# Products with 128-column weights in place of pairs of 64: v and two output projections of a MetaFormer kernel

## The chip, the core and the metric

The kernel runs on one core of a Trainium2 chip. The core has a matrix engine (TensorE, PE in the profile, with its weight loads listed apart as PEld), a vector engine (DVE), a scalar engine (ACT), GpSimd (POOL) and a sync engine (SP) that issues DMAs. Each engine works through its own queue in order; semaphores tie the queues together. The metric is the device time of one launch in microseconds, taken as the median of several runs.

A TensorE product has two operands: the weights, which a load instruction brings into the array, and the moving operand, which is streamed past them. The number of columns of the weights is the number of output partitions. The array can be used whole (weights of 128 rows by 128 columns, written 128*128 in the profile) or split into tiles, for example two halves of 64 columns each (128*64), which hold different weights.

## The reference

Input x has 32 images of 56x56 positions and 96 channels. Two layers follow, each an attention or scan part and then a feed-forward part:

```python
x = x + conv0(_ln_c(x))                  # attention in windows of 7x7, shifted by 3
t = t + ffn0(_ln_t(t))                   # rounded to fp8 and fp16, 96 -> 384 -> 96
x = x + conv1(_ln_c(x))                  # gated scan along the width
t = t + ffn1(_ln_t(t))
```

In the attention, `qkv = xs @ w_qkv + b_qkv` gives q, k and v with 3 heads of 32; each window of 49 tokens attends to itself, and the result goes through `out @ w_out + b_out`. In the scan part, a layer norm is followed by `x @ W_expand` and `sigmoid(x @ W_gate)` (192 channels each), a linear recurrence over the 56 columns of each row, the product of gate and scan, and `gated @ W_out` (192 to 96 channels). All of these are in float32.

## The kernel before

**Blocks.** Work is cut into blocks of 14 image rows, two rows of windows, 784 tokens: 4 blocks an image (NBLK), 128 in all. A block's activations `xb` lie with tokens on partitions: partitions 0 to 55 hold one image row, 64 to 119 another, and 7 such pairs of rows (G) lie side by side, each with 96 channels.

**Steps and ticks.** Each block goes through some 90 named steps (`LD`, `ma`, `q`, `v`, `pr`, `so`, ...). The string `PIPELINED` lists the steps with a lag: in tick t, step `name:lag` is run for block t - lag. A tick so has every step once, each on another block, and the steps of one engine stay in the order of this text (`in_order` ties them). The scan steps SC0 to SC5 run once for each image, spread over four ticks. TensorE's steps of a tick in order are: k, (a scan), v, pr, q, te, hf2, sc, pu2, pu1, gt1, gt0, av, hf1, tg, pu0, pu3, so, ta, tro, (scans), tf, hg2, yg, yf, hf0, hg0, hg1. The PSUM memory is used as four slots of two banks (`banks`); a slot is given back at the step that `EMPTIES` names, and that assignment is made when the program is written, not while it runs.

**The three products that change.** All contract over 128 partitions, of which 96 are channels and one is a row of ones for the bias; the other weight or activation rows are zero.

- *v* (L630 to L641). `xws` holds the normed input of the attention, channels on partitions, tokens in the order of windows: 16 windows of 49 tokens one behind the other, and 15 words of padding at the end (OVER). For each window the weights are 64 consecutive words from the window's start (49 tokens and the first 15 of the next window), the moving operand is the 96 columns of the v part of `wqkv`, and the result goes to partitions 0 to 63 or 64 to 127 of `pv`. That is 16 products a block. `xws` is written by the step `ea` (L600 to L606), two ACT copies that turn image order into window order, and is read as the moving operand by `q` and `k` (L609 to L622).
- *pr* (L785 to L795). `ot` holds the attention's output, channels on partitions, 14 rows of 56 tokens one behind the other. For each image row the weights are 64 words from the row's start, the moving operand is `wo` (96 columns), and rows of even and odd number go to the lower and upper half of the partitions. That is 14 products a block. `ot` is written by `eo` (L775 to L783).
- *so* (L985 to L998). `gTs` holds the gated scan turned to channels on partitions, 14 rows of 64 words (56 tokens and 8 of padding), in two halves of 96 channels each (h). For each row and each h there is one product, the two h adding up in PSUM. That is 28 products a block.

After v, ACT copies the result to `vs` (`ev`); after pr and so, DVE adds the result to `xb` (`ad`, `as`). A float32 product shows in the profile as two passes, each with a weight load and a matmul, so that the counts there are twice those above.

Of the kernel before, what the change touches and what calls it, by code (L numbers as in the profile page):

```python
# [8 lines left out]
F32 = mybir.dt.float32  # L9
# [8 lines left out]
C = 96  # L18
HW = 56
WS = 7  # L20
# [9 lines left out]
TP = 2 * HW  # L30
ROW = 64
# [3 lines left out]
G = 7  # L35
NBLK = 4
NTOK = G * TP
NPAIR = 8
W2 = WS * WS
OVER = 64 - W2  # L40
# [47 lines left out]
def kernel(  # L88
# [27 lines left out]
    nc = tc.nc  # L116
# [3 lines left out]
    const = ctx.enter_context(tc.tile_pool(name="const", bufs=1))  # L120
# [7 lines left out]
    def banks(name):  # L128

        slot = free.pop(0)  # L130
        (taken if tracked else free).append(slot)
        return psum.tile([128, 2, 512], F32, tag=f"ps{slot}", name=name)
# [24 lines left out]
    def zeros(size, name, first=0):  # L157
        t = const.tile([128, size], F32, name=name)
        nc.gpsimd.memset(t[first:], 0.0)
        return t  # L160
# [11 lines left out]
    for iy in range(WS):  # L172
# [12 lines left out]
    wo = zeros(C, "wo", C)  # L185

    weg = zeros(2 * E, "weg", C).rearrange("p (h m) -> p h m", h=2)
    wso = zeros(2 * C, "wso", C).rearrange("p (h c) -> p h c", h=2)
# [7 lines left out]
        fill=1.0,  # L196
# [225 lines left out]

    xws, vs, gTs, xqs = [], [], [], []
    for n in range(2):
        xws.append(const.tile([128, NTOK + OVER], F32, name=f"xw_{n}"))
        xqs.append(const.tile([128, NTOK], F8, name=f"xq_{n}"))
        vs.append(const.tile([128, NPAIR * NH, HD + 1], F32, name=f"v_{n}"))
        gTs.append(const.tile([128, 2, 8 - 2 * n, ROW], F32, name=f"gT_{n}"))
    ot = const.tile([128, NTOK + ROW - HW], F32, name="ot")
    hqs = [const.tile([128, 2 * G, ROW], F8, name=f"hq_{n}") for n in range(6)]  # L430
    qk01 = const.tile([128, 2, HALF + OVER], F32, name="qk01")
    qk2 = const.tile([128, 2, QUARTER + OVER], F32, name="qk2")
# [2 lines left out]
    fill = nc.gpsimd.memset  # L435

    def prepare_attention():
        for n in range(2):
            fill(xws[n][C:, :], 1.0)
            fill(xws[n][0:C, NTOK:], 0.0)  # L440
            fill(vs[n][:, :, HD:], 1.0)
        fill(qk2[:, :, QUARTER:], 0.0)
        fill(qk01[:, :, HALF:], 0.0)
        fill(pT[:, :, HALF:], 1.0)
        fill(ot[:, NTOK:], 0.0)
        fill(ot[C:, :], 1.0)

    ident8 = const.tile([128, TP], F8, name="ident8")

# [35 lines left out]
    def steps(*names):  # L485


        def enter(f):
            if len(names) == 1:
                step[names[0]] = f  # L490
            else:
                for k, n in enumerate(names):
                    step[n] = lambda i, k=k: f(i, k)
            return f

        return enter
# [3 lines left out]
    @steps("R0", "R1", "R2", "R3", "R4", "R5", "R6", "R7")  # L500
    def _(t, k):

        if k == 0:
            held["root", t] = epoch[0]
            epoch[0] += 1
        at = held["root", t] % 2
        st, y, v, a = stats[at], roots[at], variances[at], halfway[at]
        if k == 0:
            nc.vector.scalar_tensor_tensor(v, st[:, :, 0:G, 2], 1.0 / C, shifts, op0=ALU.mult, op1=ALU.add)
        elif k == 1:  # L510
            nc.vector.tensor_scalar(y.bitcast(I32), v.bitcast(I32), -0.5, ROOT_BITS, op0=ALU.mult, op1=ALU.add)
        elif k in (2, 5):
            nc.vector.tensor_tensor(a, y, y, ALU.mult)
        elif k in (3, 6):
            nc.vector.scalar_tensor_tensor(a, a, -ROOT_STEPS[k // 4][0], v, op0=ALU.mult, op1=ALU.mult)
        else:
            nc.vector.scalar_tensor_tensor(y, a, ROOT_STEPS[k // 5][1], y, op0=ALU.add, op1=ALU.mult)  # L517
        if k == 7:
            done[0] = held.pop(("root", t))
# [54 lines left out]
    def out_banks(name):  # L574

        po = banks(name)
        return [
            (g0, g1, po[:, k, 0 : (g1 - g0) * C].rearrange("p (g c) -> p g c", c=C))
            for k, (g0, g1) in enumerate(((0, 4), (4, G)))
        ]  # L580
# [19 lines left out]
    @steps("ea")  # L600
    def _(i):

        order = xws[i % 2][0:C, 0:NTOK].rearrange("c (r w a b) -> c r a w b", r=2, a=WS, b=WS)
        pt = held.pop(("tra", i))
        for r in range(2):
            nc.scalar.copy(order[:, r], pt[:, r].rearrange("c a (w b) -> c a w b", b=WS))  # L606

    @steps("q", "k")
    def _(i, n):  # L609

        parts, h0, h1 = ((2, 0, 2), (4, 2, 3))[n]
        size, rows = NTOK // parts, 128 // parts
        pq = banks(f"qk_{i}_{n}")
        for m in range(2):
            for j in range(parts):
                nc.tensor.matmul(  # L616
                    pq[j * rows : (j + 1) * rows, m, 0:size],
                    wqkv[:, m * C + h0 * HD : m * C + h1 * HD],
                    xws[i % 2][:, j * size : (j + 1) * size],
                    start=True,  # L620
                    stop=True,
                )  # L622
        held["qk", i, n] = pq[:, :, 0:size]
# [6 lines left out]
    @steps("v")  # L630
    def _(i):
        pv = banks(f"pv_{i}")
        for w in range(2 * NPAIR):
            p0, pair = (w % 2) * 64, w // 2
            nc.tensor.matmul(  # L635
                pv[p0 : p0 + 64, pair // 4, (pair % 4) * C : (pair % 4 + 1) * C],
                xws[i % 2][:, w * W2 : w * W2 + 64],
                wqkv[:, 2 * C : 3 * C],
                start=True,
                stop=True,  # L640
            )  # L641
        held["v", i] = pv
# [133 lines left out]
    @steps("eo")  # L776
    def _(i):
        pt = held.pop(("tro", i))
        for r in range(2):
            nc.scalar.copy(  # L780
                ot[0:C, 0:NTOK].rearrange("c (a r w b) -> c r w a b", a=G, r=2, b=WS)[:, r],
                pt[0:C, r].rearrange("c (w s) -> c w s", s=ROW)[:, :, 0:W2].rearrange("c w (a b) -> c w a b", b=WS),
            )  # L783

    @steps("pr")  # L785
    def _(i):
        parts = out_banks(f"pr_{i}")
        held["pr", i] = [(slice(g0, g1), po) for g0, g1, po in parts]
        for g0, g1, po in parts:
            for g in range(g0, g1):  # L790
                for r in range(2):
                    first = g * TP + r * HW
                    nc.tensor.matmul(  # L793
                        po[r * ROW : (r + 1) * ROW, g - g0, :], ot[:, first : first + ROW], wo, start=True, stop=True
                    )  # L795

    step["ad"] = add_out("pr")

# [185 lines left out]
    @steps("so")  # L984
    def _(i):  # L985
        held["so", i] = []
        for gT, (g0, g1, po) in zip(gTs, out_banks(f"so_{i}")):
            held["so", i].append((slice(g0, g1), po))
            for g in range(g1 - g0):
                for h in range(2):  # L990
                    for r in range(2):
                        nc.tensor.matmul(  # L992
                            po[r * ROW : (r + 1) * ROW, g, :],
                            gT[:, h, 2 * g + r, :],
                            wso[:, h, :],
                            start=(h == 0),
                            stop=(h == 1),
                        )  # L998

    step["as"] = add_out("so")  # L1000
    feed_forward("g", 1)
# [17 lines left out]
    def pipeline(text, track, one_bias):  # L1019
# [16 lines left out]
        for t in range(nblocks + 1 + max(lag for _, lag in table)):  # L1036
            if t == scans - NBLK + 1:
                parts.setdefault((t, 0), []).append(turn_toep)
            prepare(*parts.get((t, 0), ()))
            for name, lag in table:  # L1040
                i = t - lag
                if name[0:2] in ("SC", "GA"):
                    due = (i - PHASE[int(name[2])]) % NBLK == 0 and window(i)
                elif name[0] == "R":
                    due = i >= 0
                else:
                    due = (PRELOADED if name == "LD" else 0) <= i < nblocks
                if not due:
                    continue
                step[name](i)  # L1050
                if taken:
                    slots[name, i] = [len(filled[name]), list(taken)]
                    taken.clear()
                if track and name in empties:
                    use = slots[empties[name], i]
                    use[0] -= 1
                    if use[0] == 0:
                        free.extend(use[1])
            prepare(*parts.get((t, 1), ()))
# [59 lines left out]
```

## Time and profile before

| | |
|---|---|
| median of 3 runs | 3170.72 us (3163.45 to 3171.2) |
| the profiled execution | 3165.43 us, span 3163.7 us |
| mean granted TensorE clock | 0.989 |
| busy: PE, DVE, ACT, POOL | 96%, 82%, 73%, 48% |
| chain that ended last | PE 90%, ACT 5%, DVE 2% |
| of it, so (L992), pv (L635), pr (L793) | 10%, 6%, 5% |
| so: passes, mean matmul, mean weight load | 7168, 248 ns, 138 ns |
| pv | 4096, 251 ns, 138 ns |
| pr | 3584, 246 ns, 137 ns |

How to read it: the chain of work follows the last instruction back to what released it, step by step, so a share there is time that set the end. Mean times of a matmul are from its start to its modelled end and overlap with the next ones; the spacing of the starts tells the pace. In the groups, the line of a tile gives engine, operation, out<-in, the shape of the weights (rows*columns), the moving operand (rows x columns), and the number of passes. A name such as `tr_a` is the tile that is written; `pu` is the expansion and gate, `av` the attention's weighted values, `s` its scores, `py` and `ph` the feed-forward products, `tr_*` and `gt` transposes.

### The profile page before, as it was taken

The page shows a single profiled execution, that of the slowest core. Times are in us where ns is not written, and L with a number is a line of the kernel's source. Part 1 is how long each engine was busy: PE and PEld are TensorE (multiplying, and loading weights), DVE is VectorE, ACT ScalarE, POOL GpSimd, SP SyncE. Part 2 cuts the span into 40 slices and gives each one's busy share as a digit, 9 for nine tenths or more (in the row PEclk, how much of TensorE's full clock was granted, in tenths as well). Part 3 has the DMA queues.
Part 4 walks back from the last instruction along what each step waited for, and adds up shares of the span by engine and source line. Part 5 has one row for each costly group of instructions (what it writes and reads, how often), then busy time and mean ns, then how long its engine had stood idle before and what let it go on. Part 6 is the DMA issues. An engine that isn't in the chain of part 4 may idle for free.

```text
span 3163.7 us, 180034 instructions
## 1 busy us (share of the span) xinstructions
PE 3042.9 (96%) x80228; PEld 2511.5 (79%) x80228; DVE 2605.6 (82%) x7149; ACT 2304.8 (73%) x4610; POOL 1504.6 (48%) x1219
## 2 busy tenths in 40 slices
PE   4999999999999999999999999999999999999996
PEld 3778888888888888888888888888888888888875
DVE  6778888888888888888888888888888888888876
ACT  2667777777777777777777777777777777777774
POOL 4555444445444445444444444544544544544540
PEclk8899999999999999999999999999999999999998
DMA  6000111111111111111111111111111111111001
GB/s 140 23 4 19 29 32 27 29 32 27 29 32 27 28 33 27 28 33 26 27 34 27 26 34 27 26 34 27 26 33 28 27 34 27 26 32 29 23 22 34
DMA packets 232640, 97.09 MB, mean 31 GB/s; under 512 B 225292, under 2 KB 231854, under 8 KB 231854
## 3 DMA queue, kind: packets, MB, share of 16 engines
q1 hardware_dynamic: 228410, 84.40, 11.5%
q8 instruction: 633, 10.37, 1.4%
q10 hardware_dynamic: 3444, 1.06, 0.2%
q14 instruction: 153, 1.25, 0.1%
HBM read 42.05 MB, written 43.35 MB: 27 GB/s over the span
## 4 chain that ended last, share of the span: by engine, by line
PE 90%; ACT 5%; DVE 2%; issue 2%; POOL 1%; DVEq 0%; ACTq 0%; DMA 0%; SPq 0%; POOLq 0%
PE pu L896 20%; PE so L992 10%; PE qk L616 9%; PE scan L939 7%; PE av L738 6%; PE pv L635 6%; PE s L658 5%; PE pr L793 5%; PE ph_g L815 4%; PE py_f L849 4%; PE py_g L849 4%; ACT qk L628 3%; PE gt L217 3%; PE ph_f L815 3%; PE tr_f L566 2%
## 5 line engine op out<-in xcount | busy, mean ns | idle before, releaser
L896 PE MATMUL pu<-weg,xs 128*64 128x192 f32 x7168 | 640.9, 330 | 4.1 <-ACT xs L882 3.5
L535 DVE BATCH_NORM_STATS2 stats<-xb 128x6 f32<-128x192 f32 x2048 | 578.1, 348 | 1.8 <-POOL xb L871 1.7
L555 POOL TENSOR_TENSOR xn_f<-xc_f,roots 128x672 fp8e5<-128x672 f32 x128 | 243.4, 1901 | 663.6 <-DVE roots L517 663.6
L896 PEld LDWEIGHTS pu<-weg,xs 128*64 128x64 f32 x7168 | 492.4, 137 | 81.4 <-ACT xs L882 6.0
L871 POOL TENSOR_TENSOR xb<-xb,y_f 128x672 f32<-128x672 f32 x128 | 239.3, 1870 | 464.6 <-DVE y_f L867 461.2
L541 POOL TENSOR_TENSOR xc_f<-xb,stats 128x672 f32<-128x672 f32 x128 | 181.6, 1419 | 426.9 <-DVE stats L535 270.2
L628 ACT COPY qk<-qk 128x392 f32<-128x392 f32 (+1 forms) x256 | 173.8, 679 | 231.9 <-PE qk L616 231.7
L992 PE MATMUL so<-wso,gT 128*64 128x96 f32 x7168 | 322.8, 248 | 4.8 <-ACT gT L982 4.8
L827 ACT CAST h_g<-ph_g 128x784 f16<-128x784 f32 x384 | 307.6, 856 | 27.3 <-PE ph_g L815 16.9
L827 ACT CAST h_f<-ph_f 128x784 f16<-128x784 f32 x384 | 318.4, 829 | 10.4 <-PE ph_f L815 10.4
L992 PEld LDWEIGHTS so<-wso,gT 128*64 128x64 f32 x7168 | 315.9, 138 | 10.2 <-ACT gT L982 5.4
L839 POOL CAST hq<-h_f 128x784 fp8e5<-128x784 f16 x384 | 320.3, 834 | 6.1 <-DVE h_f L833 6.1
L616 PE MATMUL qk<-xw,wqkv 128*32 128x196 f32 (+1 forms) x3072 | 304.8, 392 | 2.3 <-ACT h_f L827 2.3
L606 ACT COPY xw<-tr_a 96x392 f32<-96x392 f32 x256 | 117.4, 514 | 249.1 <-PE tr_a L217 212.6
L586 DVE TENSOR_TENSOR xb<-so,xb 128x384 f32<-128x384 f32 (+1 forms) x256 | 118.1, 503 | 188.8 <-PE so L992 188.8
L586 DVE TENSOR_TENSOR xb<-pr,xb 128x384 f32<-128x384 f32 (+1 forms) x256 | 118.1, 503 | 183.4 <-PE pr L793 183.4
L959 DVE SCALAR_TENSOR_TENSOR gt<-gt,scan 128x448 f32<-128x448 f32 (+2 forms) x694 | 236.5, 400 | 38.3 <-PE scan L939 38.1
L849 PEld LDWEIGHTS <-hq 128*128 128x128 fp8e5 x5376 | 246.7, 99 | 26.4 <-DVE hq L839 8.6
L939 PEld LDWEIGHTS scan<-u,toep 64*64 64x64 f32 x12288 | 200.1, 135 | 64.6 <-ACT xw L606 29.2
L939 PE MATMUL scan<-u,toep 64*64 64x56 f32 (+1 forms) x12288 | 221.6, 220 | 30.8 <-ACT xw L606 21.3
L917 ACT COPY u<-pu 128x384 f32<-128x384 f32 (+1 forms) x512 | 242.1, 473 | 4.5 <-PE pu L896 4.5
L911 ACT ACTIVATE gt<-pu 128x384 f32<-128x384 f32 (+1 forms) x512 | 237.8, 464 | 5.5 <-PE pu L896 5.5
(161 smaller groups left out, 6706.0 us busy)
## 6 DMA issues: line engine op xcount, KB each, us to landing
xb<-in_x_dram SPq DMA_DIRECT2D x224, 126.0 KB
out_dram<-xb SPq DMA_DIRECT2D x224, 126.0 KB
taps_d<-u SPq DMA_DIRECT2D x1, 4704.0 KB
xb<-in_x_dram SPq DMA_DIRECT2D x224, 13.1 KB
xb<-in_x_dram SPq DMA_DIRECT2D x224, 7.9 KB
out_dram<-xb SPq DMA_DIRECT2D x224, 13.1 KB
out_dram<-xb SPq DMA_DIRECT2D x224, 7.9 KB
xb<-in_x_dram SPq DMA_DIRECT2D x32, 72.0 KB
```

The costliest lines, as they stand in the source:

```text
L535: nc.vector.bn_stats(st[:, g : g + 2, :].rearrange("p g s -> p (g s)"), pair.rearrange("p g c -> p c g"))
L555: engine("n" + n).tensor_tensor(xn, xc, rs[:, :, None].to_broadcast([128, G, C]), ALU.mult, **saturate)
L616: nc.tensor.matmul(pq[j * rows : (j + 1) * rows, m, 0:size], wqkv[:, m * C + h0 * HD : m * C + h1 * HD], xws[i % 2][:, j * size : (j + 1) ...
L628: nc.scalar.copy(dst, held.pop(("qk", i, n)))
L827: nc.scalar.copy(h16.rearrange("p (h t) -> p h t", h=2), held.pop(("ph", n, i, hc))[:, :, 0:HALF])
L839: engine(f"c{n}{hc}").tensor_copy(hq[:, :, 0:HW], h16.rearrange("p (r w) -> p r w", w=HW), saturate=False)
L849: nc.tensor.matmul(po[:, g - g0, :], hq[hc][:, 2 * g : 2 * g + 2, :].rearrange("p r w -> p (r w)"), w2q[:, hc, :], start=(hc == 0), stop=( ...
L871: engine("k" + n).tensor_tensor(xtiles[i], xtiles[i], held.pop(("y16", n, i)), ALU.add)
L896: nc.tensor.matmul(pu[h * RS : (h + 1) * RS, g, r * E : (r + 1) * E], xs[:, 2 * j + g, r, :], weg[:, h, :], start=True, stop=True,)
L917: nc.scalar.copy(dst, held["pu", i, j][:, 0:n, :, EH:].rearrange("p g r e -> p e g r"))
L939: nc.tensor.matmul(py[o0 : o0 + RS, b, e, rows], toep[h * RS : (h + 1) * RS, ch * HW : ch * HW + RS], u[h * RS : (h + 1) * RS, ch, rows], ...
L992: nc.tensor.matmul(po[r * ROW : (r + 1) * ROW, g, :], gT[:, h, 2 * g + r, :], wso[:, h, :], start=(h == 0), stop=(h == 1),)
```

## The change

Two tokens' rows, or two windows, are laid side by side at a distance of 64 words, so that 128 consecutive words hold both, and one product with 128-column weights takes the place of two with 64. `xws` gets 16 windows of 64 words (49 tokens and 15 of zeros), `ot` gets 14 rows of 64 words (56 tokens and 8 of zeros); `gTs` had that form already. The copies `ea` and `eo` write into the new places, and `q` and `k` read 49 of each 64 words. v then has 8 products a block, pr 7 and so 14. The order of the steps is as before on every engine, and the other instructions are the same ones; some memsets at the start are larger or smaller.

```diff
-        xws.append(const.tile([128, NTOK + OVER], F32, name=f"xw_{n}"))
+        xws.append(const.tile([128, 2 * NPAIR, 64], F32, name=f"xw_{n}"))
...
-    ot = const.tile([128, NTOK + ROW - HW], F32, name="ot")
+    ot = const.tile([128, 2 * G, ROW], F32, name="ot")
...
-            fill(xws[n][C:, :], 1.0)
-            fill(xws[n][0:C, NTOK:], 0.0)
+            fill(xws[n][C:], 1.0)
+            fill(xws[n][0:C, :, W2:], 0.0)
...
-        fill(ot[:, NTOK:], 0.0)
-        fill(ot[C:, :], 1.0)
+        fill(ot[0:C, :, HW:], 0.0)
+        fill(ot[C:], 1.0)
...
-        order = xws[i % 2][0:C, 0:NTOK].rearrange("c (r w a b) -> c r a w b", r=2, a=WS, b=WS)
+        order = xws[i % 2][0:C, :, 0:W2].rearrange("c (r w) (a b) -> c r a w b", r=2, b=WS)
...
-                    pq[j * rows : (j + 1) * rows, m, 0:size],
+                    pq[j * rows : (j + 1) * rows, m, 0:size].rearrange("p (w s) -> p w s", s=W2),
                     wqkv[:, m * C + h0 * HD : m * C + h1 * HD],
-                    xws[i % 2][:, j * size : (j + 1) * size],
+                    xws[i % 2][:, j * size // W2 : (j + 1) * size // W2, 0:W2],
...
-        for w in range(2 * NPAIR):
-            p0, pair = (w % 2) * 64, w // 2
+        for pair in range(NPAIR):
             nc.tensor.matmul(
-                pv[p0 : p0 + 64, pair // 4, (pair % 4) * C : (pair % 4 + 1) * C],
-                xws[i % 2][:, w * W2 : w * W2 + 64],
+                pv[:, pair // 4, (pair % 4) * C : (pair % 4 + 1) * C],
+                xws[i % 2][:, 2 * pair : 2 * pair + 2, :].rearrange("p w s -> p (w s)"),
                 wqkv[:, 2 * C : 3 * C],
...
-                ot[0:C, 0:NTOK].rearrange("c (a r w b) -> c r w a b", a=G, r=2, b=WS)[:, r],
+                ot[0:C, r : 2 * G : 2, 0:HW].rearrange("c a (w b) -> c w a b", b=WS),
...
-                for r in range(2):
-                    first = g * TP + r * HW
-                    nc.tensor.matmul(
-                        po[r * ROW : (r + 1) * ROW, g - g0, :], ot[:, first : first + ROW], wo, start=True, stop=True
-                    )
+                nc.tensor.matmul(
+                    po[:, g - g0, :], ot[:, 2 * g : 2 * g + 2, :].rearrange("p r w -> p (r w)"), wo, start=True, stop=True
+                )
...
                 for h in range(2):
-                    for r in range(2):
-                        nc.tensor.matmul(
-                            po[r * ROW : (r + 1) * ROW, g, :],
-                            gT[:, h, 2 * g + r, :],
-                            wso[:, h, :],
-                            start=(h == 0),
-                            stop=(h == 1),
-                        )
+                    nc.tensor.matmul(
+                        po[:, g, :],
+                        gT[:, h, 2 * g : 2 * g + 2, :].rearrange("p r w -> p (r w)"),
+                        wso[:, h, :],
+                        start=(h == 0),
+                        stop=(h == 1),
+                    )
```

## The prediction

> **What bounds the kernel now.** I read four views in this order: the page's busy shares and its chain of work, the PE timeline of one steady tick, the groups of weight loads kept apart by shape, and short windows inside single steps. The page first:
>
> ```profile
> PE 3042.9 (96%) x80228; PEld 2511.5 (79%) x80228; DVE 2605.6 (82%) x7149; ACT 2304.8 (73%) x4610; POOL 1504.6 (48%) x1219
> PE 90%; ACT 5%; DVE 2%; issue 2%; POOL 1%; DVEq 0%; ACTq 0%; DMA 0%; SPq 0%; POOLq 0%
> ```
>
> TensorE is both the busiest engine and nine tenths of the chain that ended last. So the length of its steps is what counts. The PE timeline of one tick (start, length of the union, tile, weights rows*columns, moving rows x columns, passes):
>
> ```profile
> 1501.29 2.48 PE L992 MATMUL so<-wso,gT 128*64 128x96 f32 x56
> 1503.70 0.55 PE L217 MATMUL tr_a<-ident,xc_a 56*96 56x56 f32 x14
> ...
> 1506.69 1.05 PE L849 MATMUL py_g<-w2q,hq 128*128 128x96 fp8e5 x21
> 1507.58 1.06 PE L849 MATMUL py_f<-w2q,hq 128*128 128x96 fp8e5 x21
> ...
> 1510.40 1.54 PE L635 MATMUL pv<-wqkv,xw 128*64 128x96 f32 x32
> 1511.77 1.32 PE L793 MATMUL pr<-wo,ot 128*64 128x96 f32 x28
> 1512.92 1.49 PE L616 MATMUL qk<-xw,wqkv 128*64 128x392 f32 x8
> ...
> 1522.01 0.50 PE L566 MATMUL tr_g<-ident,xn_g 128*96 128x112 fp8e5 x7
> 1522.44 2.17 PE L896 MATMUL pu<-weg,xs 128*64 128x192 f32 x24
> ```
>
> The reader is to take step lengths from start to next start: pv 1.37 us, pr 1.15, so 2.41, in all 4.93 us of a tick; a tick is 23.16 (the chain enters so at 1501.46 and again at 1524.62). An f32 product is two passes, each with its own weight load (pv x32 for 16 products). pr has 28 passes in 1.15 us: 82 ns for each pair of half-width passes, which go to the two column halves of the array and run side by side. A pass of 96 columns holds its half for nearly all of that: so's mean matmul is 248 ns, pu's with twice the columns 330, so 96 f32 columns stream for 82. Today's pace is thus set by streaming, and the loads of 64 columns lie under it.
>
> Now the loads, by shape (busy us, mean ns of one):
>
> ```profile
> L849 PEld LDWEIGHTS <-hq 128*128 128x128 fp8e5 x5376 | 246.7, 99 | 26.4 <-DVE hq L839 8.6 <-POOL hq L839 0.2
> L635 PEld LDWEIGHTS pv<-wqkv,xw 128*64 128x64 f32 x4096 | 175.6, 138 | 33.9 <-ACT h_f L827 18.1 <-issue 13.4 <-PE qk L616 0.6
> L616 PEld LDWEIGHTS qk<-xw,wqkv 128*64 128x64 f32 x1024 | 66.1, 137 | 49.7 <-issue 47.1 <-ACT h_f L827 2.5
> L616 PEld LDWEIGHTS qk<-xw,wqkv 128*32 128x32 f32 x2048 | 54.3, 111 | 47.9 <-ACT y_f L861 31.4 <-PE ph_f L815 4.1 <-issue 0.3
> ```
>
> An f32 load grows by 26 to 27 ns for 32 more columns (111 to 137 or 138), so 64 columns take some 53 ns of loading and the rest is latency. No row has an f32 load of 128 columns outside the transposes of the setup. That a load, and not the stream, can set the pace is seen in windows inside av (33 moving columns) and inside a short scan (14 moving columns), a short window beside a long one from the same start, loads counted as x:
>
> ```profile
> 1520.30:1520.50 0.20, 0.20 (x24) 1.00 0.00 0
> 1520.30:1521.30 1.00, 1.00 (x78) 1.00 0.07 16
> 126.40:126.50 0.10, 0.10 (x16) 1.00 0.00 0
> 126.40:127.10 0.70, 0.70 (x56) 1.00 0.00 0
> ```
>
> av: 54 more loads in 0.80 us, 14.8 ns each; both steps use four tiles of the array in turn, so one tile takes a new 64-column load every 59 ns. The scan: 40 in 0.60 us, 60 ns per tile, though its stream is less than half as long as av's. Two steps with unlike streams and one pace: that pace is the load's.
>
> **The change, part by part.** Per block v goes from 32 passes of 64-column weights to 16 of 128, pr from 28 to 14, so from 56 to 28: 58 pairs become 58 full-width passes that follow one another in the undivided array. They compute the same products; the moving side stays 96 f32 columns, 82 ns. The weights per pass are twice as wide.
>
> Pace of a full-width pass. From below it is the stream, 82 ns, if the load hides; from above load and stream in turn. That a load runs under a stream in the undivided array is seen in the setup's transposes (weights of up to 128 f32 columns, moving 128 and 96):
>
> ```profile
> 14.08 0.42 PE L401 MATMUL w1t<-ident,u 128*96 128x128 f32 x1
> 14.08 0.23 PEld L402 LDWEIGHTS w1t<-ident,u 96*128 96x128 f32 x1
> 14.29 0.37 PE L402 MATMUL w1t<-ident,u 96*128 96x96 f32 x1
> ```
>
> The load begins as the matmul ahead of it begins. So I take the larger of stream and load, and the load as the 59 ns of a 64-column tile plus 64 columns at 26.5 ns per 32, 53 ns: **112 ns**. Its near ends are 108 (the overhead beyond 106 almost gone) and 118 (59 doubled). The far ends are 82 and 112+82 = 194.
> - 58 x (112 - 82) = **+1.74 us** a tick.
>
> Changes of tile shape. Seven tr_g passes at 49 ns (the chain gives 0.34 us for seven of them behind matmuls of their own shape) are 0.34 us, but pu, of another shape, starts 0.43 behind: 0.09 us to change. Today v, pr and q share 128*64, and so do pu and so. Afterwards pr to q and pu to so are two more changes: **+0.18 us**.
>
> First loads that nothing hides. v's first load is already bare (1.37 - 16 x 0.082 = 0.06) and grows to 0.11: +0.05. q gets one of 0.06, so one of 0.11: together **+0.22 us**.
>
> The last passes of pr and of so now release the array after a stream of 82 instead of a pace of 112: **-0.06 us**.
>
> The copies ea and eo write runs of seven words before and after, into rows of 64 or 112 with gaps; I take nothing. ea's copy is on the chain between tr_a and the scan (0.52 us a tick), so a tenth more would cost 0.05 us, 7 us in all; a gain has no reason. The moving side of q and k is now 8 or 4 runs of 49 out of 64 in place of one run. I take nothing; above, each run breaking the stream by 2 or 3 ns over four rounds of each gives 0.12 us, 15 us in all. The larger memsets at the start are about 1100 more columns on POOL; 128x5376 took 4.58 us there, so 0.9 us, beside PE's own wait of 11.7 us for xc_a: nothing, at most 1 us. DVE, ACT, SP and the DMAs keep their instructions and order, with no new wait on any queue. Evictions behind v, pr and so (ev, ad, as) start later with PE; they have more room, because a longer tick lowers DVE's and ACT's shares. PE's waits for ACT (21.3 us for xw before the scan) remain, since tr_a comes after so and the copy only then.
>
> Sum: 1.74 + 0.18 + 0.22 - 0.06 = 2.08 us a tick. Every block passes each step once: x 128 = 266 us. All but the first few ticks have PE at nine tenths or more, so I let all of it reach the end. The profiled execution took 3165.4 us (span 3163.7 and 1.7 around it), 5.3 below the median 3170.7 of the three runs, inside their spread of 3163.5 to 3171.2. 3165.4 + 266 = **3431 us**, +8.4%.
>
> A rule that speaks harder against the change, weighed against the rows: the Trainium skill, "TensorE: Matmul & The Clock Gate", Part 3 "The mechanism", says that a weight load overlaps running matmuls only where it goes to another row group. All passes here use all rows, so by it each would pay load and stream, the 194 of rival two, and the time would be about 4040. The rows differ: so's two halves use all rows as well and keep 82 ns for a pair, where load and stream in turn would be 53 + 82 = 135. I go by the rows.
> A rule that speaks for it: "TensorEngine Tiling (Array Packing)", "Feature Incompatibilities", says that column tiling excludes the fast weight load, so the undivided array could win it back; the TensorE page, "Weight-path perf modes", says it is off for FP32. The trace shows only the fp8 side (99 ns for 128 columns). By the first alone the sum would be rival one's.
>
> **The rivals.**
> - One, *the wide load hides*. Full-width fp8 weights load in 99 ns, faster than the 64-column f32 ones at 138, so full width may have a quicker path. Against: that row's type is not f32, and f32 rows grow steadily with columns. Then the pace stays 82 and only shape changes and some bare loads are paid, 0.18 to 0.40 us a tick: 23 to 51 us, about 3205.
> - Two, *load and stream in turn* at 194: 58 x 112 + 340 = 6.84 us a tick, +875, about 4040. Against it stand so's pace and the setup's overlapped loads.
> - Three, *faster*: the undivided f32 pass streams at the pace of py, whose 21 passes of the same 96 columns take 0.89 us, 42 ns each, because the split array is what slows f32. 58 x (42 - 82) + 300 = -2.0 us a tick, -259, about 2907. The point from which it decides is a pace of 76 ns (58 x 6 pays the 0.34 of extras). Against it: py is fp8, and the undivided f32 matmuls of the setup differ by 53 ns for 32 moving columns (421 against 368), no less per column than the split ones.
>
> **How the numbers follow.** Forecast (load sets a pace of 100 to 125 ns: 3340 to 3530): 0.84; within it, 108 to 118 gives 3400 to 3480. Rival one 0.07, two 0.05, three 0.04. The predicted time is the forecast's 3431. The range 3345 to 3505 is paces of 100 to 123, and it leaves out the rivals and the top of the forecast, 2 in 10. Within 0.3%, about what a measurement of this kernel can tell from no change, only the low end of rival one could come: 0.01. Faster 0.04, slower 0.95.
>
> **What would show it.** Right: pv, pr and so at x16, x14 and x28 with 128*128 weights and f32 loads of about 190 ns (138 + 53); loads within a step about 112 ns apart; start to start pv near 1.9 us, pr near 1.6, so near 3.3 up to tr_a; pu x24 to so near 2.1; a tick near 25.2; PE still about nine tenths of the chain, DVE's share down to about 76%. Wrong: passes 82 ns apart in so (rival one), near 190 (two), or at 42 (three). The forecast also fails if q and k lengthen (runs of 49), if the copies at ea grow, or if a slower PE lets ACT's copies come earlier and PE's waits for other engines (some 70 us outside the setup, by the waits view) shrink.

## The result, and the profile after

The changed kernel takes 3426.86 us (median of five runs, 3420.41 to 3430.67) against 3170.72 for the kernel before: a ratio of 1.0804, 95% interval 1.0783 to 1.0825. That is 256 us more; the prediction said 266 more and 3431. The profiled execution has a span of 3424.5 us against 3163.7, 261 more.

The page of the kernel after, the same two lines as before the change (busy time by engine, and the chain that ended last):

```profile
PE 3303.3 (96%) x72804; PEld 2731.2 (80%) x72804; DVE 2608.6 (76%) x7149; ACT 2306.4 (67%) x4610; POOL 1503.7 (44%) x1219
PE 90%; ACT 5%; DVE 2%; issue 2%; POOL 1%; SPq 0%; DVEq 0%; ACTq 0%; DMA 0%; POOLq 0%
```

TensorE issues 7424 fewer matmuls (58 for each of 128 blocks) and is busy for 260 us longer. DVE, ACT and POOL are busy for as long as they were; only their shares fall. The chain has the same shares: nothing else became the bound. Its steps in one tick, from the PE timeline of the kernel after (start, length, line, tile, weights, moving operand, passes):

```profile
1501.21 3.37 PE L988 MATMUL so<-wso,gT 128*128 128x96 f32 x28
1504.50 0.55 PE L217 MATMUL tr_a<-ident,xc_a 56*96 56x56 f32 x14
...
1512.28 2.02 PE L634 MATMUL pv<-wqkv,xw 128*128 128x96 f32 x16
1514.14 1.73 PE L790 MATMUL pr<-wo,ot 128*128 128x96 f32 x14
1515.80 1.54 PE L616 MATMUL qk<-xw,wqkv 128*64 128x392 f32 x8
1517.26 0.55 PE L217 MATMUL tr_e<-ident,xc_e 56*96 56x56 f32 x14
...
1525.36 2.17 PE L893 MATMUL pu<-weg,xs 128*64 128x192 f32 x24
1527.46 2.81 PE L988 MATMUL so<-wso,gT 128*128 128x96 f32 x23
```

From start to next start: so 3.29 us (2.41 before), pv 1.86 (1.37), pr 1.66 (1.15), q 1.46 (1.42), pu0 and pu3 together 2.10 (2.00). That is +0.88, +0.49, +0.51, +0.04 and +0.10: 2.02 us a tick, x 128 = 259 us. A tick with one scan is 25.19 us long in the chain, against 23.16:

```profile
1527.54 3.29 PE so L988 x28
...
1552.73 3.29 PE so L988 x28
```

The 261 us of span are not all steps of the tick. In the profile after, the first k step starts 44.79 us after the span's start, and in the profile before at 38.82: 6 us are lost in the setup. From there to the end the span is 255 us longer, 2.0 us for each of 128 blocks.

The weight loads of the three steps (busy us, mean ns of one, idle before), and a short and a long window inside so (loads as x; the number behind the count is the granted clock):

```profile
L988 PEld LDWEIGHTS so<-wso,gT 128*128 128x128 f32 x3584 | 409.7, 192 | 39.9 <-issue 32.2 <-ACT gT L979 5.4 <-ACT u L914 1.1
L634 PEld LDWEIGHTS pv<-wqkv,xw 128*128 128x128 f32 x2048 | 242.7, 194 | 33.0 <-ACT h_f L824 18.1 <-issue 12.7 <-PE qk L616 0.3
L790 PEld LDWEIGHTS pr<-wo,ot 128*128 128x128 f32 x1792 | 212.3, 193 | 0.4 <-ACT y_f L858 0.4
```

```profile
1501.50:1501.70 0.20, 0.20 (x4) 1.00 0.00 0
1501.50:1504.30 2.80, 2.80 (x27) 1.00 0.03 6
```

A load of 128 f32 columns takes 192 to 194 ns, 55 more than one of 64. In so 23 loads pass in 2.60 us: a pass every 113 ns, where a pair of half-width passes took 82.

### The profile page after: what moved, and what is told of

It reads as the page before. It is cut to its first block, busy times and chain, and to the rows that moved or that the text cites. A ratio compares the mean times of both kernels' runs of the same rounds, so it can differ in the third digit from the quotient of the medians.

```text
span 3424.5 us, 165187 instructions
## 1 busy us (share of the span) xinstructions
PE 3303.3 (96%) x72804; PEld 2731.2 (80%) x72804; DVE 2608.6 (76%) x7149; ACT 2306.4 (67%) x4610; POOL 1503.7 (44%) x1219
## 4 chain that ended last, share of the span: by engine, by line
PE 90%; ACT 5%; DVE 2%; issue 2%; POOL 1%; SPq 0%; DVEq 0%; ACTq 0%; DMA 0%; POOLq 0%
PE pu L893 18%; PE so L988 12%; PE qk L616 9%; PE pv L634 7%; PE scan L936 6%; PE av L737 6%; PE pr L790 6%; PE s L657 5%; PE ph_g L812 4%; PE py_g L846 3%; PE py_f L846 3%; ACT qk L628 3%; PE gt L217 3%; PE ph_f L812 3%; PE tr_f L566 2%
## 5 line engine op out<-in xcount | busy, mean ns | idle before, releaser
L988 PEld LDWEIGHTS so<-wso,gT 128*128 128x128 f32 x3584 | 409.7, 192 | 39.9 <-issue 32.2
L988 PE MATMUL so<-wso,gT 128*128 128x96 f32 x3584 | 430.7, 278 | 4.8 <-ACT gT L979 4.8
L634 PEld LDWEIGHTS pv<-wqkv,xw 128*128 128x128 f32 x2048 | 242.7, 194 | 33.0 <-ACT h_f L824 18.1
L634 PE MATMUL pv<-wqkv,xw 128*128 128x96 f32 x2048 | 263.8, 283 | 0.0
L686 DVE SCALAR_TENSOR_TENSOR pT<-s,bias 128x392 f32<-128x392 f32 (+1 forms) x512 | 213.6, 459 | 57.1 <-PE s L657 52.7
```

The costliest lines, as they stand in the source:

```text
L634: nc.tensor.matmul(pv[:, pair // 4, (pair % 4) * C : (pair % 4 + 1) * C], xws[i % 2][:, 2 * pair : 2 * pair + 2, :].rearrange("p w s -> p ...
L988: nc.tensor.matmul(po[:, g, :], gT[:, h, 2 * g : 2 * g + 2, :].rearrange("p r w -> p (r w)"), wso[:, h, :], start=(h == 0), stop=(h == 1),)
```

## The experiments

Three theories were to be told apart. The *load theory* is that of the prediction: a full-width f32 pass waits for its own 128-column load, 112 ns, under which the stream of 82 lies. The *surcharge theory*: in the undivided array a pass costs its stream plus a fixed 30 ns, whatever is loaded. The *layout theory*: a part of the loss is that q and k read runs of 49 words and that ea and eo write elsewhere.

**The layout alone.** The kernel after, with the three products as pairs again; so for instance:

```diff
-                    nc.tensor.matmul(
-                        po[:, g, :],
-                        gT[:, h, 2 * g : 2 * g + 2, :].rearrange("p r w -> p (r w)"),
-                        wso[:, h, :],
...
+                    for r in range(2):
+                        nc.tensor.matmul(
+                            po[r * ROW : (r + 1) * ROW, g, :],
+                            gT[:, h, 2 * g + r, :],
+                            wso[:, h, :],
...
```

> The layout of the change alone: windows and rows 64 words apart, q and k reading 49 of 64 words, ea and eo writing into the new places, but v, pr and so still as pairs of half-width products. The load theory (a full-width pass waits for its 128-column f32 load, 112 ns) says the layout costs nothing: 3171 us, ratio 1.000. The layout theory (runs of 49 words break the streams of q and k, or the copies grow) says up to 22 us: 3193, ratio 1.007, and then the other parts have to be made smaller by as much.

Measured: 3169.51 us, ratio 1.0004 (0.9994 to 1.0015). The layout costs nothing that these runs can tell from zero (at most 5 us by the interval), and the layout theory falls. The loss belongs to the width of the products.

**One product at a time.** The same layout with v, pr or so alone as in the kernel after, the two others as pairs.

> The layout, with v alone at full width (8 products a block), pr and so as pairs. Load theory: 16 passes at 112 ns with a first load of 0.11 us and a change of shape to pr, 1.96 us in place of 1.37, and a bare first load in pr of 0.05: +0.64 us a tick, x 128 = +81 us, about 3252. If the cost were the shape changes and first loads alone and not the pace, +0.25 us a tick, about 3203.

> The layout, with pr alone at full width (7 products a block). Load theory: pr 1.66 us in place of 1.15, v's end 0.10 longer by a change of shape, q's first load 0.05: +0.65 us a tick, +83 us, about 3254. Shape changes and first loads alone: +0.30, about 3209. The sum over v alone and pr alone is by the load theory some 40 us more than v and pr together, since side by side they share one shape.

> The layout, with so alone at full width (14 products a block). Load theory: so 3.30 us in place of 2.41, and pu3 0.10 longer by the change of shape: +0.99 us a tick, +126 us, about 3297. Shape changes and first loads alone: +0.2, about 3197.

Measured: v alone 3251.02 us, ratio 1.0271 (1.0253 to 1.0288); pr alone 3259.01, 1.0301 (1.0282 to 1.0319); so alone 3295.90, 1.0405 (1.0388 to 1.0423). They were expected at 3252, 3254 and 3297. Against the layout alone these are +82, +90 and +126 us, 298 in all; the three together cost 257. The 40 us between belong to the border from v to pr: with one of the two at full width there is a change of shape and a bare first load, and in the change itself, where both are wide, there is neither. The PE timeline shows it; pr alone at full width, from v on:

```profile
1510.54 1.54 PE L635 MATMUL pv<-wqkv,xw 128*64 128x96 f32 x32
1512.01 1.80 PE L791 MATMUL pr<-wo,ot 128*128 128x96 f32 x14
1513.74 1.54 PE L616 MATMUL qk<-xw,wqkv 128*64 128x392 f32 x8
```

v is what it was, but pr starts 1.47 us behind it where it was 1.37: 0.10 us for the change of shape. And pr takes 1.73 us here against 1.66 behind a full-width v, since its first load is bare. With v alone at full width, v takes 1.95 us against 1.86, and pr 1.21 against 1.15. Together these are 0.32 us a tick, 41 us.

**Half the stream, the same loads, at full width.** so alone, each product cut into two of 48 moving columns:

```diff
+                for c in range(2):
+                    part = slice(c * C // 2, (c + 1) * C // 2)
                 for h in range(2):
                     nc.tensor.matmul(
-                        po[:, g, :],
+                        po[:, g, part],
                         gT[:, h, 2 * g : 2 * g + 2, :].rearrange("p r w -> p (r w)"),
-                        wso[:, h, :],
+                        wso[:, h, part],
```

> so at full width as in the run before (v and pr as pairs), and each product cut into two with 48 moving columns: 56 passes a block in place of 28, the same amount of streaming, twice the loads. Load theory: the pace stays 112 ns whatever the stream, so the step takes 0.11 + 55 x 0.112 + 0.14 = 6.4 us in place of 3.3: about 3297 + 395 = 3690. Surcharge theory (a full-width pass costs its stream plus a fixed 30 ns): 41 + 30 = 71 ns, 56 x 0.071 = 4.0 us: about 3390. Stream alone: 3300.

Measured: 4043.29 us, ratio 1.2763 (1.2721 to 1.2805). The load theory's 3690 was nearest and still 353 us short. Windows inside so and behind it (first two rows: weight loads alone; next four: PE, PEld, DVE, ACT and POOL; the number after the counts is the granted clock), and the PE timeline of the same tick:

```profile
1509.00:1509.20 0.20, 0.20 (x4) 1.00 0.00 0
1509.00:1512.00 3.00, 3.00 (x29) 1.00 0.00 0
```

```profile
1512.00:1513.50 1.50, 1.50 (x16) 1.50 (x16) 0.00 (x0) 0.00 (x0) 1.42 (x2) 1.00 0.00 0
1513.50:1515.29 1.79, 1.79 (x13) 1.70 (x14) 0.10 (x1) 0.00 (x0) 0.26 (x1) 0.53 0.00 0
1516.50:1519.00 2.50, 2.50 (x74) 2.34 (x71) 2.06 (x8) 1.22 (x4) 0.00 (x0) 0.50 0.03 7
1520.60:1523.00 2.40, 2.40 (x44) 1.80 (x40) 1.32 (x3) 2.05 (x6) 0.00 (x0) 1.00 0.00 0
```

```profile
1508.04 7.12 PE L992 MATMUL so<-wso,gT 128*128 128x48 f32 x56
1515.09 0.89 PE L217 MATMUL tr_a<-ident,xc_a 56*96 56x56 f32 x14
...
1516.56 1.97 PE L938 MATMUL scan<-u,toep 64*64 64x56 f32 x64
...
1521.00 1.06 PE L848 MATMUL py_f<-w2q,hq 128*128 128x96 fp8e5 x21
```

While the clock is whole, 25 loads pass in 2.80 us: 112 ns a pass with a stream of half the length. That is the load theory's number, and the surcharge theory's 71 ns is excluded. The 353 us have another cause, which no theory had: 5 to 6 us after so's start, in the tick shown, the granted clock falls to half, stays there for the rest of so and the steps behind it, and comes back some 7 us later. so takes 7.05 us up to tr_a in place of 6.4, and the scan behind it lasts 1.97 us against 1.16 in so alone. From so to py_f this tick takes 12.96 us. In so alone it is 7.16 (so at 1511.31, py_f at 1518.47), and the pace adds 3.1. The other 2.7 us, x 128 = 346, are nearly all of the 353. The record of the clock shows it fall 65 times in the 66 ticks between 500 and 2500 us, for 3.4, 6.8 or 10.2 us each time.

**The same cut at half width.** The layout alone with so's products as pairs, each cut into two of 48 columns:

```diff
-                            po[r * ROW : (r + 1) * ROW, g, :],
+                            po[r * ROW : (r + 1) * ROW, g, part],
                             gT[:, h, 2 * g + r, :],
-                            wso[:, h, :],
+                            wso[:, h, part],
```

> The layout alone with so as pairs of half-width products, each cut into two with 48 moving columns: 112 passes a block in place of 56. Load theory: the stream falls to 41 ns per pass and the 64-column load of 59 ns per tile sets the pace, 56 pairs x 0.059 = 3.3 us in place of 2.3: +1.0 us a tick, +125 us, about 3295. If half-width passes were always limited by streaming: no change, 3171. Against full width cut in the same way (about 3690) the half-width form should be some 395 us faster, though it issues twice as many instructions.

Measured: 3289.48 us, ratio 1.0375 (1.0349 to 1.0401), against an expected 3295; the mean clock stays at 0.989. Its windows in so, loads only:

```profile
1509.00:1509.20 0.20, 0.20 (x11) 1.00 0.00 0
1509.00:1511.00 2.00, 2.00 (x72) 1.00 0.00 0
```

61 loads in 1.80 us are 59 ns for each pair: at 48 columns the half-width form too is set by its load, and that load costs about half of the 112. A 64-column load hides under 96 moving columns and no longer under 48.

**A load of 96 columns.** so alone at full width, with 32 of the 128 weight columns left out:

```diff
-                        po[:, g, :],
-                        gT[:, h, 2 * g : 2 * g + 2, :].rearrange("p r w -> p (r w)"),
+                        po[0:96, g, :],
+                        gT[:, h, 2 * g : 2 * g + 2, :].rearrange("p r w -> p (r w)")[:, 0:96],
```

> so at full width but with weights of the first 96 columns only (32 of 128 output partitions of so are not computed, and their part of the residual addition is left out); v and pr as pairs. Same array shape, same number of passes, same stream, loads of 96 columns. Load theory: 59 + 26.5 = 86 ns a pass, so 28 x 0.086 + 0.25 = 2.6 us in place of 3.3: about 3297 - 93 = 3204. Surcharge theory, or anything else that goes by the undivided array as such: 112 ns as before, 3297 or, with the rows left out, barely less.

Measured: 3200.54 us, ratio 1.0092 (1.0065 to 1.0118), expected 3204. Its step and its load:

```profile
1501.82 2.62 PE L991 MATMUL so<-wso,gT 128*96 128x96 f32 x28
1504.37 0.55 PE L217 MATMUL tr_a<-ident,xc_a 56*96 56x56 f32 x14
```

```profile
L991 PEld LDWEIGHTS so<-wso,gT 128*96 128x96 f32 x3584 | 315.4, 165 | 39.9 <-issue 31.4 <-ACT gT L982 5.4 <-ACT u L917 1.9
```

As in so alone one product runs at a time, with as many passes and the same stream, yet the step takes 2.55 us in place of 3.29: 0.74 us for 28 passes, 26 ns a pass for 32 columns. A quarter of the columns off the load, and nearly all of the loss of pace is gone. Loads of 64, 96 and 128 columns have means of 138, 165 and 192 ns. These runs separate the number of weight columns from the stream. A result has as many partitions as its weights have columns, so no run separates the load from another cost that goes with that number; for the load speak its own records, which grow by 27 ns for 32 columns, as the pace does.

**A stream longer than the wide load.** The kernel after, with pu at full width as well (192 moving columns; the results go to other places, so that the scan works on other values):

```diff
-            for r in range(2):
-                for h in range(2):
-                    nc.tensor.matmul(
-                        pu[h * RS : (h + 1) * RS, g, r * E : (r + 1) * E],
-                        xs[:, 2 * j + g, r, :],
+            for h in range(2):
+                nc.tensor.matmul(
+                    pu[:, g, h * E : (h + 1) * E],
+                    xs[:, 2 * j + g, :, :].rearrange("p r w -> p (r w)"),
                     weg[:, h, :],
```

> The changed kernel, and in addition pu's products at full width (two rows' 64 columns side by side, 192 moving columns; its results land in other places, so what the scan reads differs). A pu pass streams for 163 ns, more than the 112 ns of a wide load. Load theory: pu's pace stays what it is, and pu3 and so now share a shape: 3427 - 10 = about 3417. Surcharge theory: 28 pairs x 0.03 = +0.84 us a tick, about 3530.

Measured: 3400.68 us, ratio to the kernel before 1.0733 (1.0698 to 1.0768), 26 us below the kernel after. The timeline:

```profile
1500.94 2.87 PE L892 MATMUL pu<-weg,xs 128*128 128x192 f32 x16
1503.73 0.89 PE L217 MATMUL gt<-ident,gt 56*96 56x56 f32 x28
...
1506.44 0.51 PE L566 MATMUL tr_g<-ident,xn_g 128*96 128x112 fp8e5 x7
1506.78 2.18 PE L892 MATMUL pu<-weg,xs 128*128 128x192 f32 x12
1508.79 3.26 PE L987 MATMUL so<-wso,gT 128*128 128x96 f32 x28
1511.98 0.55 PE L217 MATMUL tr_a<-ident,xc_a 56*96 56x56 f32 x14
```

pu2 and pu1 take 2.79 us for 16 full-width passes; before, they took 2.76 for 32 half-width ones (the chain: pu x32 for 2.75). Where the stream is the longer part, full width costs nothing, and the surcharge theory's +107 us does not come. The gain of 26 us is shape changes: tr_g to pu is 0.34 us in place of 0.43, pu to so 2.01 in place of 2.10, and so, which probably starts with its first load covered, takes 3.19 in place of 3.29, against 0.03 more in pu2 and pu1. That is 0.25 us a tick, 32 us by this tick; the expectation had counted one of these changes, and neither the one behind tr_g nor the first load.

**Is a shorter stretch enough for the clock?** v alone at full width, cut into products of 48 columns like so:

```diff
+            for c in range(0, C, C // 2):
+                first = (pair % 4) * C + c
                 nc.tensor.matmul(
-                    pv[:, pair // 4, (pair % 4) * C : (pair % 4 + 1) * C],
+                    pv[:, pair // 4, first : first + C // 2],
                     xws[i % 2][:, 2 * pair : 2 * pair + 2, :].rearrange("p w s -> p (w s)"),
-                    wqkv[:, 2 * C : 3 * C],
+                    wqkv[:, 2 * C + c : 2 * C + c + C // 2],
```

> The layout with v alone at full width (the run at 3251), and each v product cut into two with 48 moving columns: 32 passes a block at the load's pace of 112 ns, a stretch of 3.6 us a tick in which the array streams for 41 of each 112 ns. Cutting so in this way cost 350 us more than its pace accounts for, with a granted clock of 0.5 for a part of each tick. If the clock falls only after a longer stretch of such passes (so's was 6.3 us or more), v takes 0.107 + 31 x 0.112 + 0.14 = 3.7 us in place of 1.95, +1.77 us a tick, and the clock stays at 0.99: 3251 + 226 = 3477. If such a stretch of 3.6 us is enough, the mean clock is below 0.97 and the time at least 60 us above that.

Measured: 3563.31 us, ratio 1.1251 (1.1231 to 1.1271): 86 above the 3477 of the pace alone, with a mean clock of 0.964. So a stretch of 3.7 us is enough in some ticks: the record of the clock shows 34 falls in the 75 ticks between 500 and 2500 us, each for 3.4 us. In the tick where this window lies, pr and q behind v (4.18 us where they take 2.57 before) ran at a mean clock of 0.61:

```profile
1503.06:1507.24 4.18, 4.18 (x37) 2.91 (x36) 1.63 (x5) 0.80 (x1) 0.00 (x0) 0.61 0.20 50
```

The size fits: a clock of 0.964 is half rate for 2 x 0.036 x 3560 = 256 us, v alone at 3251 has 0.989 and so 72; 184 us more at half rate cost about half of that, 92. For so cut in the same way the reckoning gives more than the excess: 2 x 0.118 x 4037 = 953 us against 73, so 440 for 353. So not all of the half-rate time was lost there; why was not looked into.

**A try at a faster kernel.** The kernel before, at half width, with q moved ahead of v and pr on TensorE, and q's copy (eq) ahead of v's (ev) on ACT:

```diff
-    "... k:2 SC1:10 ne:6 ek:2 v:2 pr:3 ... ad:3 q:2 te:6 hf2:4 sf:3 ev:2 eq:2 ..."
+    "... k:2 SC1:10 ne:6 ek:2 q:2 v:2 pr:3 ... ad:3 te:6 hf2:4 sf:3 eq:2 ev:2 ..."
```

> The kernel before with one thing moved: q ahead of v and pr on PE, and eq ahead of ev on ACT, all at half width. In the kernel before, the scores wait on PE for the copy of q (the copy ends 0.12 us after PE is ready, in each tick). With q earlier the wait goes: up to 0.12 x 128 = 15 us, 3155, ratio 0.995. Against it: eq may now be behind other copies on ACT, or a PSUM slot may come free later, and the ratio is 1.000 or above.

Measured: 3257.52 us, ratio 1.0279 (1.0263 to 1.0294), a loss. The wait for q's copy is gone and longer ones took its place. Two of PE's waits (us in total, times, longest), of which the kernel before has no row, and the chain of work in one tick of this kernel (start, us, what):

```profile
PE ph_f L815 <- DVE xb L586: 68.0, 124, 0.6
PE av L738 <- ACT u L917: 16.7, 89, 0.5
```

```profile
1507.39 1.18 PE pr L793 x28
...
1508.60 0.92 DVE xb L586 x2
1509.52 1.06 DVE stats L535 x4
1510.58 0.33 DVE h_f L833
1510.90 1.06 DVE stats L535 x4
1511.96 1.22 DVE pT L687 x3
...
1514.99 1.60 PE av L738 x96
```

DVE's addition of pr to xb (ad) can only start when pr ends. PE's ph_f, two steps behind pr, now waits for that addition; in the kernel before, q's 1.4 us lay between. Everything behind it on DVE's queue is late too, with the scaling of the scores (pT) among it, and through ACT that holds up av. The two waits are 85 of the 88 us. This was the only version tried for speed, so no version here beats the kernel before.

## Why the prediction was right, point by point

- *What bounds*: right. PE keeps 90% of the chain, and the steps named are 2.02 us a tick longer, against 2.08 predicted.
- *Pace of a full-width pass, 112 ns, +1.74 us a tick*: right. Windows gave 113 in so, and 112 when the stream was halved. That the load of 128 columns could be had by adding 53 ns to the 59 of a 64-column tile is shown by three widths: 59 (half width, 48 moving columns), 84 to 86 and 112. The middle one is 19 loads in 1.60 us in the windows of the 96-column run (loads alone, below), or the 112 less the 26 of its shorter step.

```profile
1502.20:1502.40 0.20, 0.20 (x4) 1.00 0.00 0
1502.20:1504.00 1.80, 1.80 (x23) 1.00 0.00 0
```

- *Changes of tile shape, +0.18*: right, 0.10 at pu to so, and 0.10 at v to pr in the run of pr alone.
- *First loads, +0.22, and the last passes, -0.06*: together 0.16, measured a little less: with 58 x 0.030 = 1.74 and 0.20 for the shapes, 0.08 of the 2.02 us remain. v shows it: 1.86 us where 16 x 0.112 + 0.11 = 1.90. This is where most of the 10 us too much come from (0.06 x 128 = 8).
- *The time, 3431*: 4 us above the median, and a part of that is luck. The sum started from the profiled execution, 5.3 us below the median of the kernel before; from the median it would be 3437. (By the prediction's own sum its upper bound of 3505 is a pace of 122 ns, not 123.)
- *Layout, copies, waits of other engines at nothing*: right within the noise, 1.0004 for the layout alone; PE's wait for xw before the scan is 20.3 us against 21.3. *Setup at no more than 1 us*: too small in the profiles. The first k step starts at 38.8 us in both with the old layout. With the new one it starts at 41.5 to 41.6 in eight and at 44.8 in two, the change itself and the 96-column run. The larger memsets are an obvious suspect; the cause was not looked into.
- *Rival one, the wide load hides (3205)*: false; load rows of 192 to 194 ns and a pace of 113. The Trainium skill's "TensorEngine Tiling (Array Packing)", "Feature Incompatibilities", lets one hope for a fast weight load in the undivided array, by excluding it under column tiling; the f32 rows show no such thing, in line with what the TensorE page says of FP32 under "Weight-path perf modes".
- *Rival two, load and stream in turn (4040)*: false; 113 and not 194. The rule in "TensorE: Matmul & The Clock Gate", "The mechanism", that loads overlap running matmuls only in another row group, does not hold for these passes: all use all rows, and the whole stream of 82 runs under the load. (The same section also lets a load into a background weight buffer be pulled ahead of running matmuls, which these paces would fit; no run shows which it was.)
- *Rival three, faster*: false; the undivided f32 stream is as slow as the split one (pu: 16 passes in 2.79 us).

## What to carry to other kernels

Two half-width products side by side stream together and load together, each its own 64 columns (82 ns a pair, and 59 with the stream halved); one full-width product streams once but loads all 128 columns (112 to 113 ns). For f32 with 128 rows here a pass costs the longer of its stream (82 ns for 96 moving columns) and its load (59, 86, 112 ns for 64, 96, 128 columns), so joining two halves changes nothing in the pace where the stream is longer (192 columns) and loses where it is shorter. Count instructions only after that, and count each change of tile shape between neighbouring steps at 0.1 us.

## What the runs showed of the hardware that was not expected

In two runs a stretch of passes in which the stream fills little of the load's time was followed by a granted clock of half rate, though PE shows as busy without a gap. With 48 moving columns and loads of 128 (a stream of 41 ns in each 112) a stretch of 3.7 us a tick went with a mean granted clock of 0.964, and one of 6.3 us or more with 0.882, with half rate for the steps behind it too; the loss beyond the pace was 86 and 353 us. With 41 in each 59 (half width) and with 82 in each 112 (the kernel after) the mean stayed at 0.989, and the record of the clock shows no fall between 200 and 3000 us. The page "TensorE: Matmul & The Clock Gate" of the Trainium skill, Part 1, describes the gate as one that watches how busy the array is over windows of some 3.4 us and falls to half rate after an idle one. The half-rate times here, 3.4, 6.8 and 10.2 us, are multiples of such a window. That being loaded counts little, or not at all, as being busy is a reading that fits the four cases; no run singles it out. Where the limit lies between 41 of 112 and 41 of 59 was not tried.
